# A graph and attention layer on one core: keys and queries from raw rows laid out by feature, earlier edge visits, and the last chunk's node sums kept on the chip

## The chip, the cores and the metric

The kernel runs on one core of a Trainium2 chip. The metric is the time of one execution on the device in microseconds (us), the median of several runs. All data are float32.

## What is computed

There are 10,000 nodes with 512 features, and 160,000 edges sorted by their destination. Of the reference, what matters:

```python
xn = layernorm(x)
# node sums
h = xn @ W;  msgs = h[src] * edge_weight[:, None]
gnn = relu(segment_sum(msgs, dst, 10000) + bias)
# linear attention, 8 heads of 64
q, k, v = split(xn @ w_qkv.T)
q = softmax(q per head) * 64**-0.5;  k = softmax(k over all nodes)
context = k.T @ v per head;  mix = gamma_layer_norm((q @ context) @ w_out.T)
x1 = x + gnn + mix
# experts: six with 341 hidden units, weighted by one router for all rows
out = x1 + sum_e weight_e * (gelu(layernorm(x1) @ W1[e] + b1[e]) @ W2[e] + b2[e])
```

`src` lists for each edge the row that is gathered, and `dst`, sorted, the node to which it is added. The kernel sums the weighted rows of `xn` first and multiplies by W after. The destinations are drawn so that low nodes have many edges and high nodes few: a tile of 128 edges covers about 16 nodes at the end of the list.

## The kernel before

**Chunks.** The nodes are cut into 19 chunks of 512 and a last one (chunk 19) of 272. A chunk lies in SBUF as 128 partitions (68 in the last) by SUB = 4 rows by 512 features. A float32 product with 512 columns is two matmul instructions in the profile.

**Start.** `normal_rows` (L411) loads chunks of x on SP's queue (L416), takes their statistics on DVE (L166, L167), finishes the factors on POOL, normalises on ACT (L422) and stores the normalised rows to `xn_d` in DRAM (L424). It is called in portions from `work`, so that all 20 chunks pass while PE does chunks 0 and 1; ROWS_IN sets the pace. After LISTS = 10 chunks, `edges_listed` (L445) loads the lists of the edges and `place_edges` (L454), a generator, computes on DVE at which row of its window each edge adds. Two of its steps follow each chunk of rows.

**Keys and queries.** The loop at L856 goes over the chunks. It needs the rows turned (features on the partitions): `turned_rows` (L837) calls `transposed` (L196), 16 transposes on PE (L201) and four evictions (L203), on ACT alone for the first two chunks and then two on ACT and two on DVE. Chunks 0 and 1 use plain products (`times`, L209). From chunk 2 on, `seven` (L246) makes keys and queries together from 28 products per chunk, with sums of the turned rows (`xs_b`, L226 to L229) and of the weights (`kq_sum`, L233 to L236). ACT takes the exponentials (L885, L896 to L901) with the factor `usable`, which is 1 when a test of the weights' norms holds (`norms`, `as_they_are`). Then 16 products `pc` (L911) add the keys' transposed rows times the normalised rows into `G` (L914, L918), and the queries are turned (16 transposes) and stored as `qT_d`. The rows for `pc` are loaded again from `xn_d` (`rows_of`, L834).

**Edge visits.** The 1250 edge tiles belong to 866 windows of 32 node rows, four windows to a group, 217 groups. The first 384 windows have two tiles each (groups 0 to 95), the others one. `edges_in` (L573) issues one gather of 128 rows per tile on POOL (L583) and builds `sel` on DVE (L589, L591). `edges_summed` (L595) does a visit: eight or four products of 32 output rows each into one bank (L601), a copy on ACT (L604) and one store of 128 rows to `part_d` on ACT's queue (L605). Windows overlap in up to four rows, which `carry` (L672) adds from each window to the next by accumulating transfers within DRAM on POOL's queue (L673). The order of PE's instructions is written out by hand: `work(us)` counts the nominal time of the products done and calls `edges_to` for as many tiles as PACE = 0.9 us (later ROW_PACE = 0.96 us) allows. The count starts at -16 tiles when chunk 2 begins. Gathers use a ring of 24 buffers. The other engines' order comes from a scheduler that goes by a cost model; `behind` adds to it that one instruction comes after another.

**Node rows.** Behind a short stage that forms the matrix `mix`, the loop at L1063 goes over the chunks again. `attention` (L1038), three chunks ahead (MIXED = 3), multiplies queries with `mix` (`po`), takes a layer norm and adds x. `gathered` (L1013) fetches a chunk's node sums from `part_d` with an indirect transfer on POOL (L1017); which windows have to be carried by then is in AT_HAND. The sums are turned (`aT`), multiplied with W (`pg`), and bias, relu and the sum follow on DVE (L1089, L1090). When chunk 16 calls `gathered(17)`, groups 207 to 210 are forced; chunk 17 begins with `all_edges_in` (L1005), which forces groups 211 to 216, carries the last windows and releases the edges' memory; then come the attention of chunk 19 and the rest.

**Experts.** `experts_weights` (L293) loads their weights on SP, `sums_of_weights` (L379) adds parts of them on DVE. The first chunk's normalised and turned rows are made while chunk 18 is worked on (`rows_in`, L351, L367, and the sums `xs`, L233 to L236). From the first expert product (L243) to the end PE runs without the edges.

A second path for edge lists that do not fit these windows (`general_path`, L710) is taken when a count of good edges, made with `place_edges`, is short of its full value.

## Time and profile before

| | us |
|---|---|
| median of 3 runs | 3510.95 (3510.28 to 3531.97) |
| the profiled execution | 3518.48, of which its span 3516.7 |
| start, to the first product of chunk 2 | 160 |
| keys and queries of chunks 2 to 19, to the last product of `seven` | 1024 |
| end of that, general path's test, `mix`, first attention | 159 |
| node rows of chunks 0 to 16 | 673 |
| node rows to the end, forced visits, to the first expert product | 127 |
| experts | 1374 |

The profiled execution was on its own run, 7.5 us above the median. Start and end of a stage are read from PE's timeline. "Busy" is the time in which an engine executes; issuing a transfer is not counted. In a row of a group, the number after the bar is the idle time of the engine just before these instructions, with what ended it; "issue" is idle time for which the profile shows no wait.

### The profile page before, as it was taken

Reading aid. Unit: us, or ns where it says so; the run is one execution under the profiler, and the core shown is the slowest. Engines: PE = TensorE matmul, PEld = TensorE weight load, DVE = VectorE, ACT = ScalarE, POOL = GpSimd, SP = SyncE. Lnnn points to the kernel's source line nnn. Section 1 sums busy time; section 2 is a strip of 40 time slices with the busy share of each in tenths; the row PEclk is TensorE's granted clock in tenths of the full one; section 3 lists DMA queues with packets and bytes.
Section 4 is the critical chain, followed back from the end, with each engine's and each line's share of the span. In section 5 each row is a group of like instructions: output and inputs, shape, how many; then the busy total and the mean of one; then the engine's idle time right before and its main releaser. Section 6 shows DMA issues by size and latency. Waiting matters only on the chain. (4 is left out here: it accounts for less than half of the span.)

```text
span 3516.7 us, 36142 instructions
## 1 busy us (share of the span) xinstructions
PE 3256.7 (93%) x12819; PEld 1916.0 (54%) x12819; DVE 1766.5 (50%) x3902; ACT 831.1 (24%) x1674; POOL 1311.2 (37%) x1421
## 2 busy tenths in 40 slices
PE   6899998988999989898998988999999999999998
PEld 3433333333333333333333335888888888888886
DVE  6644445444444425564565557445445544544542
ACT  5321212121112112121222113222222222222221
POOL 3466666665666656676676630000000000000000
PEclk8999999999999979899999988999999999999999
DMA  9677777776777878898998882221212212122111
GB/s 392 235 217 249 227 247 248 254 223 208 227 223 243 247 275 318 313 332 293 318 336 301 294 268 61 60 75 58 60 57 76 60 49 84 49 60 73 60 37 38
DMA packets 216735, 654.39 MB, mean 186 GB/s; under 512 B 34425, under 2 KB 74361, under 8 KB 188831
## 3 DMA queue, kind: packets, MB, share of 16 engines
q0 software_dynamic: 104096, 354.29, 32.0%
q1 hardware_dynamic: 69992, 175.33, 15.2%
q10 hardware_dynamic: 42452, 122.31, 9.0%
q8 instruction: 105, 1.72, 0.2%
q14 instruction: 90, 0.74, 0.1%
HBM read 491.21 MB, written 166.63 MB: 187 GB/s over the span
## 5 line engine op out<-in xcount | busy, mean ns | idle before, releaser
L583 POOL DMA_INDIRECT msg<-xn_d,src_sb x1250 | 1229.9, 984 | 634.4 <-issue 287.2
L601 PE MATMUL pm<-msg,sel 128*32 128x512 f32 x2504 | 351.7, 617 | 54.5 <-issue 44.5
L911 PE MATMUL pc<-xn,ek 128*128 128x512 f32 (+1 forms) x640 | 306.5, 624 | 20.5 <-issue 15.0
L209 PE MATMUL po<-G,qT 128*128 128x512 f32 (+1 forms) x640 | 302.0, 613 | 13.0 <-issue 12.2
L209 PE MATMUL pg<-wq,aT 128*128 128x512 f32 (+1 forms) x640 | 301.3, 617 | 10.2 <-issue 9.0
L604 ACT COPY part<-pm 128x512 f32<-128x512 f32 x217 | 127.1, 586 | 733.9 <-PE pm L601 276.0
L601 PEld LDWEIGHTS pm<-msg,sel 128*32 128x32 f32 x2504 | 66.1, 110 | 302.7 <-issue 266.2
L209 PEld LDWEIGHTS pg<-wq,aT 128*128 128x128 f32 (+1 forms) x640 | 117.7, 192 | 195.7 <-issue 184.7
L911 PEld LDWEIGHTS pc<-xn,ek 128*128 128x128 f32 (+1 forms) x640 | 122.7, 199 | 177.4 <-issue 164.7
L209 PEld LDWEIGHTS po<-G,qT 128*128 128x128 f32 (+1 forms) x640 | 117.4, 191 | 185.6 <-issue 181.4
L243 PE MATMUL px<-xnT,w_sb 128*128 128x256 f32 (+1 forms) x800 | 204.6, 379 | 6.8 <-DVE u L1290 6.8
L243 PE MATMUL p<-kq_sum,xs_b 128*128 128x512 f32 (+1 forms) x432 | 201.4, 600 | 3.2 <-issue 2.4
L166 DVE BATCH_NORM_STATS2 st<-ot 128x6 f32<-128x512 f32 (+1 forms) x160 | 110.3, 689 | 178.5 <-issue 119.2
L243 PE MATMUL px<-w_sb,hh 128*128 128x256 f32 (+1 forms) x800 | 185.7, 379 | 0.0
L243 PE MATMUL py<-xs,w_sum 128*128 128x256 f32 (+1 forms) x800 | 185.3, 374 | 0.0
L243 PE MATMUL p<-wk,xnT 128*128 128x512 f32 (+1 forms) x288 | 148.1, 637 | 34.9 <-issue 26.7
L243 PE MATMUL py<-w_sum,hh 128*128 128x256 f32 (+1 forms) x800 | 179.2, 379 | 0.0
L589 DVE TENSOR_TENSOR sel<-iota_w,place 128x128 f32<-128x128 f32 (+2 forms) x217 | 74.5, 344 | 206.1 <-remote 86.2
L243 PEld LDWEIGHTS px<-xnT,w_sb 128*128 128x128 f32 x800 | 150.7, 192 | 29.9 <-DVE u L1290 10.0
L243 PEld LDWEIGHTS py<-w_sum,hh 128*128 128x128 f32 (+1 forms) x800 | 150.0, 188 | 22.7
L243 PEld LDWEIGHTS px<-w_sb,hh 128*128 128x128 f32 (+1 forms) x800 | 150.0, 188 | 22.7
L243 PEld LDWEIGHTS py<-xs,w_sum 128*128 128x128 f32 x800 | 149.8, 190 | 19.9
(298 smaller groups left out, 4577.4 us busy)
## 6 DMA issues: line engine op xcount, KB each, us to landing
part_d<-part ACTq DMA_DIRECT2D x217, 256.0 KB
msg<-xn_d,src_sb POOLq DMA_INDIRECT x1250
xn<-in_x SPq DMA_DIRECT2D x19, 1024.0 KB
xn_d<-xn ACTq DMA_DIRECT2D x19, 1024.0 KB
qT_d<-qT ACTq DMA_DIRECT2D x19, 1024.0 KB
qT<-qT_d SPq DMA_DIRECT2D x19, 1024.0 KB
xt<-in_x SPq DMA_DIRECT2D x19, 1024.0 KB
x_d<-ot SPq DMA_DIRECT2D x19, 1024.0 KB
```

The costliest lines, as they stand in the source:

```text
L166: nc.vector.bn_stats(st[:r, s, :], t[:r, s, :])
L209: nc.tensor.matmul(po[:r, :], t[:, kb, s * r : (s + 1) * r], w[:, kb, :], start=kb == 0, stop=kb == KB - 1)
L243: nc.tensor.matmul(o, lhs[j], rhs[j], start=start and j == 0, stop=stop and j == n - 1, skip_group_check=True)
L583: nc.gpsimd.indirect_dma_start(out=m[k], out_offset=None, in_=xn_d, in_offset=bass.IndirectOffsetOnAxis(ap=src_sb[:, t0 + k : t0 + k + 1], ...
L589: nc.vector.tensor_tensor(sel[:, :n], iota_w[:, None, :].to_broadcast([P, n, WIN]), place[:, t0 : t0 + n, None].to_broadcast([P, n, WIN]), ...
L601: nc.tensor.matmul(pm[h * WIN : (h + 1) * WIN, :], sel[:, k, :], m[k] if k < len(m) else m[0], start=j == 0, stop=j == batch - 1, skip_gro ...
L604: nc.scalar.copy(part, pm)
L911: nc.tensor.matmul(pc, ek[:r, s, cb * P : (cb + 1) * P], xn[:r, s, :], start=s == 0, stop=s == SUB - 1)
```

## The change

- The turned rows are no longer made on PE. The host hands in x a second time, laid out by feature and chunk (`x_t`), and a chunk's turned raw rows are one load of 1 MB on SP (`turned_rows`), into the same single buffer. Raw rows give the right products because the weights are centred on the chip (`centred`: four products with a matrix of ones and four DVE instructions for each of the two), and because ACT's factor becomes the row's own one over its deviation (`rate`, `rates`).
- At the start the keys' weights and the first turned rows are loaded ahead of x; ROWS_IN is 2.0, LISTS 18. The steps of `place_edges` no longer follow the chunks of rows: the first comes after the last statistics, one later step after the last softmax of chunk 1. The reload of chunk 2 comes after the last load of x. The count of visits starts at -11 tiles.
- Windows from 384 on store 24 rows instead of 32: one transfer per window, four per group. The eight rows left out are cleared once, at chunk 5 (`rest_cleared`, 16 transfers). The test of the edges follows (USED).
- The gather of node sums is put after the last asked gather of edges (`behind`).
- Groups 211 to 216 keep their sums in SBUF (`parts`); those from 214 on are not stored. Chunk 19's node sums are made by products of these with a matrix that says which row belongs to which node (`numbered`, `last_sums`): four groups after chunk 17, two groups and the gathered rows (zeros, unless the general path ran) in chunk 19. The last carry ends at window 853.
- The attention of chunk 19 comes at chunk 16, as the distance of three has it, with visits beside it. After chunk 17 come the last groups, and then the experts' first rows are loaded ahead of their weights. The sums of the experts' weights come after the first rows are turned and before chunk 19's bias.

The diff, cut to its core:

```diff
+USED = 24
-ROWS_IN = 1.6
-LISTS = 10
+ROWS_IN = 2.0
+LISTS = 18
+FIRST_SUMS = 4
-           (17, 788), (18, 820)]
+           (17, 788), (18, 820), (19, 853)]
...
+        def turned_rows(c):
+            xnT = b_io.tile([P, KB, SUB * P], F32, name="xnT")
+            nc.sync.dma_start(xnT[:, :, : SUB * chunks[c][1]], columns(x_t, c))
+            return xnT
+
+        def centred(w):
+            pcol = psum.tile([P, D], F32, name="pcol", tag="ps")
+            for kb in range(KB):
+                nc.tensor.matmul(pcol, all_ones, w[:, kb, :], start=kb == 0, stop=kb == KB - 1)
+            for kb in range(KB):
+                nc.vector.scalar_tensor_tensor(w[:, kb, :], pcol, -1.0 / D, w[:, kb, :], op0=ALU.mult, op1=ALU.add)
...
+        nc.sync.dma_start(wk, w_qkv_t[:, D : 2 * D].rearrange("(k p) d -> p k d", p=P))
+        xnT = turned_rows(0)
+        nc.sync.dma_start(wq, w_qkv_t[:, :D].rearrange("(k p) d -> p k d", p=P))
+        squared = [squares_of(wk, "qT"), squares_of(wq, "xs_b")]
+        centred(wk)
         normal_rows(2)
...
-            nc.scalar.dma_start(part_d[i * P : (i + 1) * P, :], part)
+            if batch > 1:
+                nc.scalar.dma_start(part_d[i * P : (i + 1) * P, :], part)
+            elif i < STORED:
+                for h in range(GROUP):
+                    nc.scalar.dma_start(by_window[i * GROUP + h, :USED, :], part[h * WIN : h * WIN + USED, :])
...
+        def rest_cleared():
+            zero = pools["w"].tile([P, PER, D], F32, name="none", tag="on", bufs=1)
+            nc.gpsimd.memset(zero, 0.0)
+            for w in range(PAIRED, STORED * GROUP, P):
+                end = min(w + P, STORED * GROUP)
+                for q in range(USED, WIN, PER):
+                    nc.scalar.dma_start(by_window[w:end, q : q + PER, :], zero[: end - w])
...
-            nc.sync.dma_start(xn[: chunks[c][1]], tokens(xn_d, c))
+            load = nc.sync.dma_start(xn[: chunks[c][1]], tokens(xn_d, c))
+            if c == KEPT:
+                behind(load, last_load[0])
...
-                for _ in placing[0]:
-                    pass
+                for step in placing[0]:
+                    if step:
+                        behind(step, last_softmax[0])
-                done[1] = -16 * PACE
+                done[1] = -11 * PACE
...
-                            nc.scalar.activation(o[:r, at, :], po[:r], AF.Exp, scale=usable[:r])
+                            nc.scalar.activation(o[:r, at, :], po[:r], AF.Exp, scale=rate[:r, at : at + 1])
...
             if c + 1 == EARLY:
                 normal_rows(NCH)
+                behind(next(placing[0]), last_stats[0])
                 xn_next = rows_of(c + 1)
             if c + 1 < NCH:
-                xnT = turned_rows(c + 1, xn_next)
+                xnT = turned_rows(c + 1)
...
+        def last_sums(o, mine, groups, at):
+            n = SUB * chunks[-1][1]
+            for kb in range(KB):
+                kbs = slice(kb * P, (kb + 1) * P)
+                pt = psum.tile([P, SUB * P], F32, name="pt", tag="ps")[:, :n]
+                for g in groups:
+                    nc.tensor.matmul(pt, parts[g // 3][:, g % 3, kbs], mine[:, g].rearrange("p s n -> p (s n)"),
+                                     start=g == groups[0], stop=at is None and g == groups[-1], skip_group_check=True)
+                if at is None:
+                    nc.scalar.copy(o[:, kb, :n], pt)
+                    continue
+                r = chunks[-1][1]
+                for s in range(SUB):
+                    nc.tensor.matmul(pt[:, s * r : (s + 1) * r], at[:r, s, kbs], ident[:r, :r],
+                                     start=False, stop=s == SUB - 1, skip_group_check=True)
+                nc.vector.tensor_tensor(o[:, kb, :n], o[:, kb, :n], pt, ALU.add)
...
+            behind(sums, held["asked"])
...
-            if c == NCH - 3:
-                all_edges_in()
-                ats += [gathered(c + 1), gathered(c + 2)]
-            if c + MIXED < NCH - 1:
+            if c + MIXED < NCH:
                 mixed.append(attention(c + MIXED, nodes_rows))
-            elif c == NCH - 3:
-                mixed.append(attention(NCH - 1, nodes_rows))
+            elif c < NCH - 1:
+                nodes_rows()
             else:
-                nodes_rows()
+                last_sums(aT, mine, range(FIRST_SUMS, NQ - ON_CHIP), at)
...
+            if c == NCH - 3:
+                limit[0] = ON_CHIP + FIRST_SUMS
...
             if c == NCH - 3:
-                sums_of_weights()
+                mine = numbered()
+                aT_last = io.tile([P, KB, SUB * P], F32, name="aT_last", tag="ot", bufs=MIXED + 2)
+                edges_to(limit[0])
+                last_sums(aT_last, mine, range(FIRST_SUMS), None)
+                rows_first = all_edges_in()
```

## The prediction

> **What bounds the kernel now.** I read the page first, then busy time by stage, then the groups of PE instructions, then PE's timeline at the two places where it stands still, and there POOL's and SP's.
>
> The page: PE is the engine.
>
> ```profile
> PE 3256.7 (93%) x12819; PEld 1916.0 (54%) x12819; DVE 1766.5 (50%) x3902; ACT 831.1 (24%) x1674; POOL 1311.2 (37%) x1421
> DMA  9677777776777878898998882221212212122111
> ```
>
> The busy time by stage (columns: window, its length, then busy us of PE, PEld, DVE, ACT and POOL, granted clock, DMA share, GB/s). I cut at the first product of chunk 2 (160), the last chunk's key products (1184), the first chunk with node sums (1343), the node products of the 17th chunk (2016) and the first expert product (2143):
>
> ```profile
> 0.00:160.00 160.00, 111.43 (x339) 58.98 (x340) 105.78 (x301) 81.48 (x117) 52.75 (x102) 0.86 0.80 318
> 160.00:1184.00 1024.00, 939.22 (x3396) 384.80 (x3394) 478.72 (x961) 198.51 (x321) 664.64 (x684) 0.97 0.75 235
> 1343.00:2016.00 673.00, 620.41 (x2141) 234.34 (x2144) 382.87 (x993) 139.95 (x270) 462.86 (x464) 0.96 0.90 314
> 2016.00:2143.00 127.00, 97.35 (x337) 39.20 (x330) 82.18 (x183) 24.52 (x56) 35.76 (x76) 0.88 0.76 229
> 2143.00:3517.00 1374.00, 1351.62 (x6146) 1145.85 (x6145) 660.44 (x1338) 360.71 (x866) 0.00 (x0) 0.99 0.19 58
> ```
>
> PE idles 48.6 us before 160 and 29.7 us between 2016 and 2143, much more per us than elsewhere. The last 1374 us are the experts, full and not touched. In the key stage the removed instructions are one row (window 184 to 1184), and their 33.4 us busy and 3.8 us idle belong to PE, the bound:
>
> ```profile
> L201 PE MATMUL pt<-ident,xn 128*128 128x128 f32 (+1 forms) x272 | 33.4, 273 | 3.8 <-issue 3.8
> L911 PE MATMUL pc<-xn,ek 128*128 128x512 f32 x544 | 256.5, 614 | 20.5 <-issue 15.0 <-DVE sel L591 1.7 <-DVE G L914 1.6
> ```
>
> The start, PE's timeline (start, length, in brackets the idle time before and who ended it): long stalls, all for the turned rows or for VectorE:
>
> ```profile
> 13.28 0.47 PE L201 MATMUL pt<-ident,xn 128*128 128x128 f32 x1 [13.28 <-ACT xn L422]
> 31.72 5.91 PE L209 MATMUL pk<-wk,xnT 128*128 128x512 f32 x8 [13.29 <-ACT xnT L203]
> 51.99 0.56 PE L632 MATMUL pn<-n_small,all_ones 128*128 128x1 f32 x2 [5.94 <-DVE mv L167]
> 100.73 0.90 PE L201 MATMUL pt<-ident,qt 128*128 128x128 f32 x3 [13.32 <-DVE G L918]
> ...
> 159.87 1.88 PE L243 MATMUL p<-kq_sum,xs_b 128*128 128x512 f32 x4
> ```
>
> Behind it, in the timelines of POOL and of SP's queue: the gathers start when the last chunk of `xn_d` is stored, and SP issued the last x load only after the reload of chunk 2 (L834), which waited for a buffer until 113.89:
>
> ```profile
> 149.77 1.26 POOL L583 DMA_INDIRECT msg<-xn_d,src_sb  x1 [13.24 <-DMA xn_d<-xn]
> ...
> 113.89 0.33 SPq L834 DMA_DIRECT2D xn<-xn_d  x1
> 114.33 0.82 SPq L416 DMA_DIRECT2D xn<-in_x  x1
> ```
>
> The end, again PE's timeline: the last ten groups are forced in two heaps, each waiting for gathers or for the copy of a sum, and then the experts wait for VectorE:
>
> ```profile
> 2029.07 1.49 PE L601 MATMUL pm<-msg,sel 128*32 128x512 f32 x8 [2.47 <-ACT part L604]
> 2033.89 1.93 PE L601 MATMUL pm<-msg,sel 128*32 128x512 f32 x8 [3.32 <-issue]
> 2057.26 1.93 PE L601 MATMUL pm<-msg,sel 128*32 128x512 f32 x8 [3.65 <-issue]
> 2064.32 4.15 PE L601 MATMUL pm<-msg,sel 128*32 128x512 f32 x24 [5.12 <-ACT part L604]
> 2142.57 2.04 PE L243 MATMUL px<-xs,w_sum 128*128 128x256 f32 x4 [13.68 <-DVE xs L235]
> ```
>
> **What the Trainium skill says.** "DMA: Bandwidth & Descriptors", the section on why a DMA increments its semaphore by 16: a transfer runs on the largest k up to 16 that divides its slowest dimension, and on the hardware path on the lowest-numbered k engines. 24 rows give k = 12: two rows per engine and transfer, eight per group of four transfers, which is what 128 rows over 16 engines give. So engines 0 to 11 are relieved of nothing by the smaller stores; the trace of before has no 24-row store to show it. The same page, queues and rings: each DMA engine goes round between the queues that have work, so the burst of clearing stores shares with the gathers and does not stop them. "TensorE: Matmul & The Clock Gate", Part 1: an idle window halves the clock. The trace agrees: 0.86 granted before 160 and 0.88 in the end stage against 0.99 for the experts. Same page, the spec table: ACT and DVE queues are strict FIFO, so what stands ahead in them delays PE's evictions; the 13.32 us for G's copy, whose product had ended at 87.4, show it.
>
> **The change part by part**, against the profiled execution (3518.5 us, span 3516.7).
>
> Raw rows by feature, key stage. Out go 16 transposes per chunk (1.8 us by the timeline) and four evictions of about 0.6 us, half ACT's, half DVE's. By the row above that is 37.2 us of PE for 17 chunks. In comes one 1 MB load per chunk on SP. Its buffer is free when the seven products of the chunk end; until the next chunk PE has 16 `pc` products (13.8 us), 16 `qt` transposes (1.8) and a visit or two (1.9 each): 17 to 19 us. The load I estimate at 7 to 10 us, by the 6.5 to 7.8 us that the `z_d` stores of the same size take in the chain of waits, plus contention; the four `xs_b` sums after it are 2.7. It fits; on SP nothing that PE needs sooner stands behind it. If the cover were gone, PE would wait for the rest of it in each of 18 chunks. It adds 18 MB in 1024 us, 18 GB/s on 235, so the DMA share goes from 0.75 to about 0.81. POOL issues a gather per 1.25 us (2000.33, 2001.58 and on in its timeline). A chunk takes 58.4 us (270.76 to 329.11) and asks for 40.6 tiles (36.5 us of nominal work at 0.9 each), 50.8 us of POOL; at 56.3 a chunk it still has slack. I take 34 us of the 37 (bounds 15 and 42).
>
> Start. PE no longer waits for a row chunk, its statistics, its normalisation and 16 transposes: it needs the keys' weights and the turned rows, the first loads now. The first load landed at 7.5 us, so PE starts near 8 instead of 32. PE's work to 160, summed from the timeline, is 114 us; less 8.5 of transposes, plus 7 for centring (8 products of 0.86 us): 112. From 8 this ends at 120; the norm test (6) and two waits for VectorE to centre (3 each) make 132. VectorE's queue stands against it: 105.8 us busy before 160, and the placing of the edges (some 20 us in its timeline) now comes after the last statistics, just where `kq_sum` and `xs_b` are needed. If all of that placing comes first, chunk 2 starts at 146; I take 138, a gain of 22 (bounds 10 and 32). The gathers have to start sooner too, as visits come five tiles (4.5 us of work) earlier: the last x load no longer stands behind L834, and I expect the first gather at 135 to 143.
>
> Late stores. Four issues on ACT of 0.33 us instead of one, 118 groups (96 to 213): 0.98 us more per group, 116 us of ACT's queue in the row stage, where ACT is busy 140 of 673 us. PE has six banks between itself and ACT and two for visits, 4.6 us apart, so I take 0, with bounds of -5 and +25. Bytes saved, 7.7 MB, are written instead as 16 clearing stores of 512 KB at chunk 5: 20 us of all engines at 390 GB/s, a quarter of which is spare. I take +3 (0 to 10).
>
> End. Chunk 19's attention now comes one chunk earlier with its visits beside it, so by the pacing rule groups 207 to 214 fall between products and only 215 and 216 are forced. Of 29.7 us idle I let 24 go, and 2 of the slow clock (`pg` took 16.0 us at 2035.75 against 13.9 at 2083.93). New on PE: 24 products of 272 columns at 0.857 x 272/512 = 0.46 us, 10.9; the ones that add the gathered rows, 2.4 against the 1.2 of the transposes they replace. Sum: 26 less, 12 more: -14 (bounds -24 and +4). Late next is VectorE, with about 19 us of work (turning 2.3, sums 2.8, weight sums 6, statistics) against 21 of PE. The wait of chunk 18 for its gathered rows hides the carry (6.1 us from issue to the gather) and the gather behind 10 us of products and 7.3 of the first node sums.
>
> Sum: -34 - 22 + 0 + 3 - 14 = -67: 3451.5 in the profile. The profiled execution was 7.5 us above the median of the runs, 3510.95, so the forecast is 3444.
>
> **Rivals.** (1) The key stage gives nothing: PE waits there for something else at the same rate (it idles 8% there, mostly "issue"), and the extra DMA traffic slows gathers. For: DMA share up, POOL at 87% of its rate. Against: the row stage idles the same 8% at a share of 0.90. Then -36 + 3 = -33: 3478. (2) Slower: ACT's queue. Place: the row stage; four issues per group ahead of the copies of `po`, `aT` and `part`. If 0.9 us of each group's 0.98 reached PE, it would be +106 - 67: 3550. It beats the gain from 0.57 us per group, and is a loss of over 1% from 0.87. Against: ACT idles 79% there. (3) More: the start at 128, all of the end's idle time gone, the stalls of the key stage shrunk with fewer evictions: -105, 3406. (4) It doesn't do what it says: one row past the 24th in a late tile would send the kernel down the general path, thousands of us. I worked out the reference's edges: the highest place in a late tile is 23 (rows 0 to 23), so it isn't taken.
>
> **How the numbers follow.** Forecast 0.60, (1) 0.17, (2) 0.07, (3) 0.15, (4) 0.01. The range drops the slower case and takes in (1) and (3): 3404 to 3488. One per cent, about what a measurement tells from no change, is 35 us: the forecast, (3) and two fifths of (1) are faster, the rest of (1) the same, with some of the forecast's spread: faster 0.81, same 0.12, slower 0.07.
>
> **What would show it.** No `pt<-ident,xn` row; PE's count near 12,580 (336 transposes out, 96 products in). First product of chunk 2 near 138, first gather by 143. The key stage near 990 us. Row stage within 10 of 673. No idle over 6 us between the node products of chunk 17 and the first expert product. Wrong if PE waits at the seven products for the turned rows (the load isn't hidden), if `aT` or `part` copies appear as releasers in the row stage, or if PE idles over 15 us before chunk 2 for `place` or `xs_b`.

## The result, and the profile after

The kernel after takes 3550.6 us (median of 10 runs, 3537.67 to 3556.44), the kernel before in the same comparison 3518.61 (3507.34 to 3531.97): a ratio of 1.0085, 95% interval 1.0064 to 1.0106. A second comparison gave 1.0074 (1.0050 to 1.0098). The forecast was 3444. The runs that follow were spread over several chips: the kernel before takes 3510 to 3522 on most of them and 3299 on one, so every time stands beside the kernel before of its own comparison. Where one run of a kernel is all there is, the text says so.

The profiled execution of the kernel after took 3556.44 us with a span of 3554.6; before it was 3518.48 and 3516.7. The page, the lines that answer to those of before:

```profile
PE 3245.7 (91%) x12579; PEld 1895.3 (53%) x12579; DVE 1744.4 (49%) x3905; ACT 803.5 (23%) x1630; POOL 1308.3 (37%) x1424
DMA  9587777887777778899898865212112122122111
```

PE has 240 instructions fewer, as counted ahead, but only 11.0 us less busy time. The busy time by stage, cut at the first product of chunk 2, at the seven products of chunk 19, at the first node product, at the node products of chunk 15 and at the first expert product (columns as before: window, length, busy us of PE, PEld, DVE, ACT, POOL, granted clock, DMA share, GB/s):

```profile
0.00:173.00 173.00, 114.77 (x306) 58.80 (x307) 113.25 (x333) 76.44 (x107) 40.19 (x98) 0.82 0.79 314
173.00:1221.00 1048.00, 917.04 (x3125) 356.63 (x3124) 459.24 (x923) 180.86 (x288) 675.69 (x692) 0.94 0.78 255
1401.00:2044.00 643.00, 594.67 (x2033) 223.19 (x2034) 353.14 (x943) 128.67 (x254) 439.03 (x442) 0.96 0.90 305
2044.00:2177.00 133.00, 123.86 (x441) 54.84 (x441) 81.94 (x190) 26.21 (x59) 46.86 (x87) 0.96 0.73 209
2177.00:3555.00 1378.00, 1351.49 (x6146) 1145.22 (x6144) 668.95 (x1361) 360.29 (x867) 0.00 (x0) 0.99 0.20 60
```

The start is longer (173 us against 160) and the key stage is longer (1048 against 1024), at a lower granted clock (0.82 against 0.86, and 0.94 against 0.97), although PE has fewer instructions in both (306 against 339, 3125 against 3396). The row and end stages can't be read off against the windows of before: their cuts at 1343 and 2016 lie ahead of the first node product (1359.0) and among the node products of chunk 15, which begin at 2002.7.

For all that follows I cut every kernel at the same five places of PE's timeline: the first of chunk 2's seven products, that of chunk 3, the first node product (`pg`) of chunk 0, that of chunk 15, and the first expert product. "Stretch" is the time from chunk 3 to the first node product; it holds the key stage from chunk 3 on and the short stage that forms `mix`. Row stage and end follow. us:

| kernel, profiled execution | chunk 2 starts | chunk 2 | stretch | row stage | end |
|---|---|---|---|---|---|
| before | 159.9 | 50.5 | 1148.6 | 643.7 | 139.9 |
| before, once more (b_again) | 160.2 | 49.7 | 1139.4 | 646.1 | 138.8 |
| after | 173.0 | 65.4 | 1162.5 | 642.9 | 133.0 |
| after, once more (after_again) | 174.3 | 67.1 | 1146.3 | 649.9 | 127.5 |

b_again and after_again ran beside each other. Against before, the two pairs say: start +13 and +14, chunk 2 +15 and +17, stretch +14 and +7, row stage -1 and +4, end -7 and -11, experts +4 and +2. Of the stages, only the end is shorter in both pairs.

PE's timeline at the start of the kernel after (start, length, in brackets the idle time before and who ended it):

```profile
80.95 0.45 PE L217 MATMUL pt<-ident,qt 128*128 128x128 f32 x1 [10.62 <-DVE stats L183]
...
157.19 0.45 PE L217 MATMUL pt<-ident,qt 128*128 128x128 f32 x1 [15.69 <-DVE qt L210]
...
173.03 1.88 PE L259 MATMUL p<-kq_sum,xs_b 128*128 128x512 f32 x4
...
217.91 4.52 PE L985 MATMUL pc<-xn,ek 128*128 128x512 f32 x6 [17.77 <-ACT ek L969]
```

PE does start at 9.8 us, and has the keys and queries of chunk 0 by 63. What it gained it gives back at the query transposes of chunks 0 and 1, which wait for the softmax on VectorE (24.4 and 20.5 us in four waits each, of which the first is shown). In chunk 0 the softmax stands in VectorE's queue behind the statistics of rows that are still being loaded; in chunk 1 behind the placing of the edges, which now begins after the last statistics. The queues of SP and POOL show why rows and gathers are late:

```profile
63.50 0.33 SPq L457 DMA_DIRECT2D xnT<-in_x_t  x1
...
147.40 1.32 POOL L626 DMA_INDIRECT msg<-xn_d,src_sb  x1 [0.19 <-issue]
173.77 0.96 POOL L626 DMA_INDIRECT msg<-xn_d,src_sb  x1 [25.05 <-DVE count L557]
```

The turned rows of chunk 1 have to wait for the one buffer until chunk 0's products end, and the loads of x stand behind that wait on SP. The first gather comes at 147, and the second 26 us later: the message buffers lie where the placing's temporaries were, and the last of these is read by L557. Chunk 2's first visit then waits for its messages, and the copies and exponentials queued behind it hold PE for 17.8 us at 217.91.

In the key stage, the row of the removed transposes is gone, and the idle time has moved to `pc`. The same group in both kernels, from the seven products of chunk 3 to those of chunk 19 (busy, mean ns, then idle before and its releasers), before and after:

```profile
L911 PE MATMUL pc<-xn,ek 128*128 128x512 f32 x512 | 242.4, 615 | 20.5 <-issue 15.0 <-DVE sel L591 1.7 <-DVE G L914 1.6
```

```profile
L985 PE MATMUL pc<-xn,ek 128*128 128x512 f32 x513 | 251.1, 633 | 52.9 <-issue 21.8 <-ACT ek L969 14.2 <-ACT ek L970 10.2
```

The end is as drawn up, with one stall above the 6 us that I allowed:

```profile
2111.51 5.52 PE L225 MATMUL pg<-wq,aT 128*128 128x512 f32 x8 [6.32 <-DVE ot L1201]
...
2129.56 7.50 PE L1114 MATMUL pt<-mine,parts 128*128 128x272 f32 x32
...
2176.80 1.03 PE L259 MATMUL px<-xs,w_sum 128*128 128x256 f32 x4
```

### The profile page after: what moved, and what is told of

The parts are those of the page before. It is cut to its first block, busy times and chain, and to the rows that moved or that the text cites. A ratio compares the mean times of both kernels' runs of the same rounds, so it can differ in the third digit from the quotient of the medians.

```text
span 3554.6 us, 36005 instructions
## 1 busy us (share of the span) xinstructions
PE 3245.7 (91%) x12579; PEld 1895.3 (53%) x12579; DVE 1744.4 (49%) x3905; ACT 803.5 (23%) x1630; POOL 1308.3 (37%) x1424
## 4 chain that ended last, share of the span: by engine, by line
PE 53%; DMA 4%; issue 3%; DVE 2%; another core or an unknown queue 1%; ACT 0%; ACTq 0%; SPq 0%; DVEq 0%
PE px L259 14%; PE pz L259 10%; PE py L259 9%; PE po L225 7%; PE pg L225 7%; PE pm L644 3%; PE ph L259 2%; DMA z_d<-xt 1%; PE pt L217 1%; DMA xt<-x_d 1%; DMA xt<-in_x 0%; DMA xn<-x_d 0%; DMA w_sb<-in_w 0%; DVE xt L1460 0%
## 5 line engine op out<-in xcount | busy, mean ns | idle before, releaser
L644 PE MATMUL pm<-msg,sel 128*32 128x512 f32 x2504 | 342.9, 610 | 26.9 <-issue 22.9
L225 PE MATMUL po<-G,qT 128*128 128x512 f32 (+1 forms) x640 | 309.2, 626 | 12.3 <-issue 11.3
L225 PE MATMUL pg<-wq,aT 128*128 128x512 f32 x608 | 285.8, 615 | 15.1 <-issue 7.3
L259 PE MATMUL px<-xnT,w_sb 128*128 128x256 f32 (+1 forms) x800 | 205.1, 379 | 12.1 <-DVE u L1398 12.1
L225 PEld LDWEIGHTS pg<-wq,aT 128*128 128x128 f32 x608 | 111.9, 193 | 188.4 <-issue 167.2
```

What stands on the lines that cost most here:

```text
L225: nc.tensor.matmul(po[:r, :], t[:, kb, s * r : (s + 1) * r], w[:, kb, :], start=kb == 0, stop=kb == KB - 1)
L259: nc.tensor.matmul(o, lhs[j], rhs[j], start=start and j == 0, stop=stop and j == n - 1, skip_group_check=True)
L644: nc.tensor.matmul(pm[h * WIN : (h + 1) * WIN, :], sel[:, k, :], m[k] if k < len(m) else m[0], start=j == 0, stop=j == batch - 1, skip_gro ...
```

## Experiments

### Are the clearing stores or the small stores the loss? (a_full)

```diff
-            if batch > 1:
+            if i < STORED:
                 nc.scalar.dma_start(part_d[i * P : (i + 1) * P, :], part)
-            elif i < STORED:
-                for h in range(GROUP): ...
...
-                rest_cleared()
```

> The kernel after, with the late groups storing all 128 rows in one store and no clearing stores. Theory A (the 16 clearing stores, which run at 166 to 220 us beside the first gathers, make the messages of the first visit land late): the 17.8 us idle of PE in chunk 2 goes, the seven products of chunk 3 start some 15 us earlier than at 238.4, and the kernel takes about 3533. Theory B (the messages are late because the gathers themselves start late, the second of them at 173.8 behind the placing of the edges): chunk 2 keeps at least 12 us of its idle time, and the kernel stays within 5 us of 3550. If the four small stores per group cost something in the row stage, that stage (first node product of chunk 0 to that of chunk 15, 642.9 us) gets shorter by over 5 us; I expect within 3.

Measured: 3551.78 us, 1.0107 of before (1.0067 to 1.0147), and chunk 2 took 67.6 us with an idle 18.5 us at `pc`, as in the kernel after. Theory A falls and B holds: the clearing stores, which run beside chunk 2's products, cost nothing that can be seen, and the late messages come from the late gathers. The row stage took 636.9 us, 6.0 less than in the kernel after; the kernel after itself differs by 7.0 between two executions, so that says nothing.

### The placing as before (a_start, a_start2)

```diff
-ROWS_IN = 2.0
-LISTS = 18
+ROWS_IN = 1.6
+LISTS = 10
...
                     placing.append(place_edges(*edges_listed()))
+                for _ in range(2 if placing else 0):
+                    next(placing[0], None)
...
-                for step in placing[0]:
-                    if step:
-                        behind(step, last_softmax[0])
+                for _ in placing[0]:
+                    pass
...
-                behind(next(placing[0]), last_stats[0])
```

> The kernel after, with the placing of the edges as the kernel before has it (lists loaded at the 10th chunk, two placing steps per chunk of rows, no order behind the last statistics and the last softmax); the turned rows, the clearing and the end stay. Theory S (the placing that was moved behind the last statistics holds the softmax of chunk 1 and the message buffers): the 15.7 us wait of PE at the query transposes of chunk 1 goes, the second gather comes at about 150 instead of 173.8, chunk 2 starts at 150 to 158, and the kernel takes 3515 to 3535. Rival (the start is bound by the loads of x and the statistics, so that chunk 1 waits anyway): chunk 2 starts at 165 or later and the kernel is within 8 us of 3550.

> The earlier run with before's placing of the edges in the kernel after, again, beside the kernel after itself: 15 to 30 us less than the kernel after, of which the idle time in chunk 2 is 15; chunk 2 itself still starts at 170 to 175, because VectorE places the edges while chunk 0's softmax waits.

Measured: 3522.5 us, 1.0021 of before (1.0003 to 1.0039), and the second time 3523.35, 1.0031 (1.0013 to 1.0048), beside 1.0074 for the kernel after on the same chip: 18 us less. The gathers run without a gap from 140.7 us on, and chunk 2 takes 47.9 and 47.7 us; its idle time is gone. But chunk 2 still starts at 173.0 and 172.3. Half of theory S held: the gathers and the time, not the start. The rival was right on the start and wrong on the time: VectorE now places edges at 62 to 113 us, and PE waits 36.1 us in chunk 0 for the softmax. In both orders of the placing VectorE has the same work before chunk 2, and starting PE 22 us sooner brought nothing by itself.

### The two kernels once more, side by side (after_again, b_again)

No edit: the kernel after and the kernel before as they stand, in one comparison with a_start2.

> The kernel after, unchanged, on the same chip as the three other runs, because the kernel before took 3515 in one comparison and 3299 in another. If the loss is that of the start (chunk 2 at 173 instead of 160, its first visits 15 us late for messages) and the key stage can't repay it since the gathers set its pace, the ratio to before is 1.005 to 1.010 where before takes 3515, and 1.000 to 1.006 where it takes 3299. Rival: where gathers are quick (3299) the removed transposes count in full and the ratio falls to 0.990 or lower.

> The kernel before, unchanged, for its stage times on the chip of these runs: chunks 3 to 18 in 974 us and the row stage in 644 where the kernel takes 3515; 830 to 845 and 570 to 580 where it takes 3299.

Measured: 3541.34 us and, in one run, 3509.98, beside 3512.56 for before: the ratio of 1.0074 is in the range expected where before takes 3515. The rival speaks of the other chip and is not tested here. The stages of the table above repeat within 3 us up to chunk 2. From chunk 3 on two executions of one kernel differ by up to 16 us in the stretch, so that a difference of a few us there is not read as an effect.

### Does the removal of the transposes count without the gathers? (n_before, n_after)

```diff
-                    if k < n:
+                    if k < n and t0 + k >= 24:
+                        m[k] = kept[(t0 + k) % 24]
+                    elif k < n:
                         m[k] = pools["m"].tile([P, D], F32, name="msg")
+                        kept[(t0 + k) % 24] = m[k]
```

> The kernel before with only the first 24 of the 1250 gathers of messages; later visits multiply the messages of these 24 tiles again. All products, copies and stores stay. Theory G (in the key stage PE waits for messages, a wait that the records of PE hide): chunks 3 to 18 (973.7 us from the seven products of chunk 3 to those of chunk 19) take under 920. Rival P (PE itself is the bound there): over 950.

> The kernel after with only the first 24 gathers of messages, as in the run beside it. Theory G: chunks 3 to 18 (982.5 us in the kernel after) take 30 to 40 us less than in the kernel before without its gathers, so the removed transposes count in full once no message is waited for. Rival P (the gain was eaten by the order on ACT and DVE or by the load of the turned rows): within 12 us of the kernel before without its gathers.

Measured, in one run each: 3234.45 and 3235.65 us, where the kernel before takes 3514.8. The gathers cost 280 us, far more than any stage of the change was to bring. The stretch of both, by engine:

```profile
208.00:1175.50 967.50, 963.64 (x3764) 405.09 (x3760) 522.80 (x1065) 223.54 (x362) 5.25 (x5) 1.00 0.23 83
```

```profile
232.60:1176.60 944.00, 937.30 (x3505) 378.51 (x3503) 504.92 (x1027) 205.32 (x329) 5.26 (x5) 1.00 0.29 102
```

Without gathers PE is full and its clock is 1.00. Chunks 3 to 18 take 828.4 us before and 802.1 after: 26.3 less, short of the 30 to 40 that theory G named and well above the 12 of rival P. It is what PE's busy time in the stretch falls by (963.64 to 937.30), so the removal is worth what PE saves, once PE is what counts. Of theory G the numbers came near; that PE's loss is a wait for messages is not shown by these runs, and a later experiment speaks against it. The stretch is 23.6 shorter and the end 2.3, which pays for the start (13.9 later) and chunk 2 (10.7 longer): the change is even.

### The start as before, raw rows from chunk 2 on (a_mid, a_best)

```diff
+        normal_rows(2)
         wk = kvp.tile([P, KB, D], F32, name="wk")
...
-        xnT = turned_rows(0)
...
+        xnT = early_rows(0, xn)
...
-                xnT = turned_rows(c + 1)
+                xnT = early_rows(c + 1, xn_next) if c + 1 < EARLY else turned_rows(c + 1)
```

`early_rows` is `transposed` from the normalised rows; chunks 0 and 1 have the factor `usable` again; and the placing is that of before. a_best also centres `wq` before chunk 0's products.

> The kernel after with the start of the kernel before: chunks 0 and 1 take their turned rows from the normalised rows by 16 transposes each, rows are loaded first, the edges are placed between the statistics; raw rows by feature are used from chunk 2 on, and the weights are centred while PE waits for the first rows. Theory L (the change lost because its start puts the gathers and chunk 2 late; the key stage gains once the gathers start at 140 to 150 as before): chunk 2 starts at 157 to 163, chunks 3 to 18 take 940 to 960 us, and the kernel 3485 to 3500. Rival M (the supply of messages sets the pace of the key stage, so that nothing is gained there whatever the start): chunks 3 to 18 take 965 to 980 and the kernel 3505 to 3520.

> The earlier run with the start of the kernel before (raw rows by feature from chunk 2 on), with the weights for the queries centred too while PE waits for the first rows: chunk 2 starts at 158 to 164 instead of 168, and the kernel takes 10 us less than the run with before's placing, 0.5% to 0.9% less than before. If the start doesn't matter since the gathers set the pace from then on, it equals the run with before's placing within 4 us.

a_mid ran on the chip where before takes 3298.81: 3285.33 us, a ratio of 0.9956 (0.9940 to 0.9973). Chunk 2 started at 168.1, later than expected, and chunks 3 to 18 took 826.0. Theories L and M were put in numbers of the other chips, so this run doesn't decide between them. a_best ran on a chip where before takes 3512.56: 3521.21, 1.0037 (1.0017 to 1.0057), with chunk 2 at 166.0 and a stretch of 1140.3. So a_mid beats the kernel before by 13.5 us on the one chip, and a_best loses 8.7 to it on the other. There it equals a_start2 within 4 us, as its second expectation said: a start that is 6 us sooner is gone by the end. The kernel after itself wasn't run on the first chip, so the sign of the whole change there is open.

### What of the gathers sets the pace? (g64_before, b16, a_once; then b16_2, g64_2, a_once2)

```diff
-                            out=m[k], out_offset=None, in_=xn_d,
-                            in_offset=...(ap=src_sb[:, t0 + k : t0 + k + 1], axis=0))
+                            out=m[k][:64], out_offset=None, in_=xn_d,
+                            in_offset=...(ap=src_sb[:64, t0 + k : t0 + k + 1], axis=0))
```

```diff
-tc.tile_pool(name="edge_m", bufs=24,
+tc.tile_pool(name="edge_m", bufs=16,
```

```diff
-                xnT = turned_rows(c + 1)
+                xnT = turned_rows(c + 1) if c < EARLY else xnT
```

The first and second are edits of the kernel before, the third of a_start.

> The kernel before with each gather fetching 64 of its 128 rows and each node product multiplying those 64 rows only: as many GpSimd instructions and products as before, half of the gathered bytes and packets. If the issue of one gather per 1.25 us on GpSimd sets the supply, chunks 3 to 18 (973.7 us before, 828.4 without gathers) stay over 930. If the fetching and landing sets it, they fall under 880.

> The kernel before with 16 message buffers instead of 24. If the buffers set the supply (a gather can start only when a group of eight has been multiplied), chunks 3 to 18 take over 1030 us instead of 973.7. If the DMA's or GpSimd's own rate sets it, under 990.

> The kernel of the earlier run with before's placing (chunks 3 to 18 in 954.1 us), with the turned rows loaded for chunks 0 to 2 only; later chunks multiply those of chunk 2 again, so 17 loads of 1 MB are left out. If these loads hold up the messages or come late for the sums, chunks 3 to 18 take under 938 us. If they cost nothing, within 8 us of 954.

All three, one run each, fell on the chip where before takes 3298.81. Chunks 3 to 18 took 828.2, 843.0 and 836.4 us. With no gathers at all PE needs 828.4 for the first two and 802.1 for the third, which has no transposes. Where the gathers cost so little, these runs can't tell what of them costs. Again, one run each, on chips where before takes 3515 and 3522:

> The kernel before with 16 message buffers instead of 24, again, for a chip on which the kernel before takes 3515 (there GpSimd stays 16 gathers ahead of the group being summed). If a message can be used only some 20 us or more after its gather, chunks 3 to 18 take over 1050 us instead of 972; if PE is held up by something that the lead of the gathers doesn't touch, under 990. On a chip of the other kind: 843 again.

> The kernel before with 64 of 128 rows fetched by each gather and multiplied, again, for a chip on which the kernel before takes 3515: if bytes and packets set the pace, chunks 3 to 18 take under 900 us instead of 972; if the number of gathers does, over 950. On a chip of the other kind: 828 again.

> The same kernel with all gathers, and with the turned rows loaded for chunks 0 to 2 only (17 loads of 1 MB left out), on a chip where before takes 3515: if these loads eat the gain of the removed transposes, the stretch from chunk 3 to the first node product falls from 1143 to 1150 to under 1130; if not, it stays within 10 us of 1146. On a chip where before takes 3300, 990 again.

Measured: a stretch of 1134.3 with 16 buffers, 1161.4 with half of the rows, 1148.8 without 17 MB of turned rows, against 1139.4 and 1148.6 before and 1142.6 and 1150.1 in a_start. Chunks 3 to 18 took 973.6 with 16 buffers and 988.0 with half of the rows, as expected if neither the lead of the gathers nor their bytes set the pace. Within the 16 us by which two executions differ, neither buffers nor bytes nor the new loads set it. The part of rival (1) that blamed the extra DMA traffic is out.

### Gathers that nobody waits for (n_side, n_side_after)

```diff
+                    if k < n and t0 + k < 8:
+                        m[k] = kept[t0 + k] = ...   # gathered once, multiplied in every visit
+                    elif k < n:
+                        beside = pools["m"].tile([P, D], F32, name="msg")
+                        m[k] = kept[(t0 + k) % 8]
+                        nc.gpsimd.indirect_dma_start(out=beside, ...)
```

> The kernel before with all gathers issued, but the products multiply the messages of the first eight tiles, so that from then on neither PE waits for a gather nor a gather for PE (16 buffers that nobody reads). Theory W (PE loses its time by waiting for messages): chunks 3 to 18 take 825 to 850 us although the gathers now run at full rate, one per 1.25 to 1.4 us. Theory C (the traffic of the gathers slows PE itself, its operands or its clock): over 900 where the kernel before takes 3515.

> The same edit in the kernel after. Theory W: 20 to 30 us less in chunks 3 to 18 than in the run beside it. Theory C: within 12 us of it.

Measured, in one run each: 4742.72 and 4702.53 us, beside 3514.69 for before. Chunks 3 to 18 took 2016.5 us in n_side and 1921.2 in n_side_after. Theory W falls, and C holds in that PE itself is slowed; but its number (over 900) is left far behind, and the second run is 95 us below the first where C said within 12 and W 20 to 30. Two windows of n_side, one with gathers and one without, while GpSimd stands for 708 us in a carry that waits for the stores to `part_d`:

```profile
700.00:1000.00 300.00, 87.64 (x107) 22.25 (x108) 16.20 (x28) 6.37 (x10) 230.95 (x215) 0.50 0.68 193
1900.00:2200.00 300.00, 300.00 (x1168) 126.06 (x1161) 162.04 (x323) 67.04 (x108) 0.00 (x0) 1.00 0.19 71
```

In 300 us PE gets 107 product instructions done beside 215 gathers, and 1168 without. No product waits for a gather here. The timelines of PE and of POOL at the beginning of that:

```profile
203.65 1.01 PE L919 MATMUL pc<-xn,ek 128*128 128x512 f32 x1 [1.79 <-issue]
205.75 1.01 PE L919 MATMUL pc<-xn,ek 128*128 128x512 f32 x1 [1.09 <-issue]
208.55 1.01 PE L919 MATMUL pc<-xn,ek 128*128 128x512 f32 x1 [1.79 <-issue]
```

```profile
204.49 0.95 POOL L590 DMA_INDIRECT msg<-xn_d,src_sb  x1 [0.31 <-issue]
205.74 0.95 POOL L590 DMA_INDIRECT msg<-xn_d,src_sb  x1 [0.30 <-issue]
```

PE's idle time is put down to "issue", that is to nothing that the profile shows. The DMA engines are on average less busy (0.68) than in the row stage (0.90), which speaks against DMA engines that are full. In the kernels before and after, GpSimd pauses when the ring of 24 buffers is full: in before's stretch 137.8 us of its idle time end with a visit. In n_side, up to the carry, it is never idle for more than 0.9 us. The two engines then fall into step, here a little later, PE and POOL:

```profile
765.75 1.01 PE L919 MATMUL pc<-xn,ek 128*128 128x512 f32 x1 [1.79 <-issue]
768.55 1.01 PE L919 MATMUL pc<-xn,ek 128*128 128x512 f32 x1 [1.79 <-issue]
```

```profile
765.35 1.10 POOL L590 DMA_INDIRECT msg<-xn_d,src_sb  x1 [0.30 <-issue]
766.75 1.10 POOL L590 DMA_INDIRECT msg<-xn_d,src_sb  x1 [0.30 <-issue]
768.15 1.10 POOL L590 DMA_INDIRECT msg<-xn_d,src_sb  x1 [0.30 <-issue]
```

A product starts every 2.80 us and a gather every 1.40: one product for two gathers. From 600 to 1000 us there are 143 products beside 286 gathers, and from 1000 to 1400 again 143 and 286.

### One gather in six left out (a_45)

```diff
-                    if k < n:
-                        m[k] = pools["m"].tile([P, D], F32, name="msg")
+                    if k < n and k and (t0 + k) % 5 == 4:
+                        m[k] = newest
+                    elif k < n:
+                        m[k] = newest = pools["m"].tile([P, D], F32, name="msg")
```

An edit of a_start, with all its visits and products. Meant was one gather in five; since the first gather of a visit always stays, 207 of the 1250 are left out, one in six.

> The kernel after with before's placing of the edges (1143 and 1150 us from chunk 3's seven products to the first node product, 944 in the kernel after without gathers), with one gather in five left out; the visit multiplies the message fetched just before in its place. If each gather costs PE the same, 121 fewer of some 604 save a fifth of the 200 us: 1105 to 1115. If PE is held up only when GpSimd gets no pause, the pauses grow and the stretch falls under 1060. If the number of gathers doesn't matter, it stays over 1135. On a chip where before takes 3300 it tells less: 950 to 985.

Measured, in one run: 3280.73 us beside 3522.29 for before. The stretch of a_start and of a_45:

```profile
220.90:1363.50 1142.60, 1021.59 (x3505) 398.99 (x3503) 499.12 (x1026) 200.73 (x325) 743.21 (x760) 0.94 0.78 258
```

```profile
216.10:1204.70 988.60, 955.61 (x3504) 380.92 (x3502) 498.53 (x1026) 201.66 (x329) 620.18 (x626) 0.98 0.79 263
```

POOL has 134 instructions fewer and the stretch 154.0 us less, 1.15 us for each, at the same DMA share. That is no price per gather: all the other 621 cost only 44.6 us more (n_after, 944.0), as PE is nearly full again (955.61 of 988.60 busy). The row stage falls from 632.9 to 572.3, near the 561.8 without gathers. The second of the three expectations held (under 1060), and the first, that a gather costs PE its share of the loss, some 0.3 us, did not.

The second gave a reason: PE is held up when GpSimd gets no pause. The traces fit it. In the stretch, n_after, a_start and a_45 have the same products in the same order, so each can be set beside n_after in steps of eight products. a_start is behind by over 2 us in 31 steps of 437, which make 157 of its 199 us; a_45 in 6, which make 29 of its 45. So the loss comes in short standstills. And a_start has 30 runs of 14 or more gathers that follow each other within 2 us each, a_45 has 6. That such a run brings on the standstill is not shown by this.

## Why the prediction was wrong

Two steps failed, each worth about half of the 105 us between forecast and measurement: that PE bounds the key stage, so that its saved work is saved time (48 us), and that PE's own work sets the start (50 us).

**What bounds the kernel.** I read "PE is the engine" from its 93%, and found POOL at 87% of its rate with "still slack". Between chunk 3 and the first node product, time went with the gathers, not with PE's work: on the chips where before takes 3510 to 3522 the stretch has 755 to 760 POOL instructions in before, after, a_full, a_start, a_start2, a_once2 and a_best and lasts 1139 to 1163 us, with the transposes and without. With 626 it lasts 988.6, with next to none 944.0 or 967.5. POOL is not the bound in PE's place: at 1.25 us each, 757 instructions are 946 us of the 1148.6. PE's 93% was partly work and partly products that stood in PE without getting on: PE was busy 1042.4 us in before's stretch and 963.6 in that of n_before, which has the same products.

**Key stage, -34.** PE does save the work, and it is worth 26.3 us in chunks 3 to 18 when nothing is gathered, inside my bounds of 15 to 42. With gathers I measured +9 (973.7 to 982.5) and, in the second pair, -7 (970.9 to 964.2). This is rival (1), to which I gave 0.17: PE stays at the same rate for another reason. My reason in it, more traffic, was wrong (a_once2); the argument that I set against it, the same 8% idle at a DMA share of 0.90 in the row stage, was no argument, since the row stage loses 82 us to the gathers too (643.7 against 561.8).

**Start, -22.** This is the other step that failed: wrong by 35 us, and by 50 with chunk 2. I summed PE's work and added small waits. The worry that I named, placing in front of `kq_sum` and `xs_b`, was put at 8 us. I missed two waits: the softmax of both early chunks behind statistics and placing on VectorE (44.9 us together), and the message buffers behind the placing's last temporary (25.05 us at the second gather). "First gather by 143" was 147.40, and the second is what counted. The test I gave, "PE idles over 15 us before chunk 2 for `place` or `xs_b`", nearly met the place: 15.69 us, for the softmax behind `place`. a_start shows that the placing's order costs 18 us of the result. The other part, a start of PE that brings nothing, stays.

**Clearing, +3, late stores, 0.** Right. a_full is not faster than the kernel after, and the row stage is 642.9 and 649.9 us against 643.7 and 646.1. The row stage is within the 10 us that I allowed, though not read between the cuts of 673: my "17th chunk" at 2016 is the 16th, whose node products begin at 2002.7. My place for the clearing was wrong: the scheduler put it beside chunk 2, not at chunk 5. Rival (2), with ACT's queue as the cause of a loss at 3550, gave the measured time by luck, with a mechanism that didn't happen: in the row stage `part` shows nowhere as a releaser of PE, and `aT` once for 1.1 us, in the kernel before just the same.

**End, -14.** -6.9 and -11.3, with less DVE stall at the first expert product (13.68 us gone) and the two heaps of forced groups gone. Without gathers the end gains only 2.3, so here too part of what went was waiting that comes with the gathers. The experts, which I had called untouched, take 4 and 2 us more: their waits for `u` on VectorE grew from 6.8 to 12.1 us, in the second pair from 6.7 to 11.7.

**The sum** of -67 was to give 3451.5 in the profile, and the profiled execution took 3556.44. The 105 us between them are the start and chunk 2 (50), the stretch (48), the end (7), the experts (4), less 3 for the clearing, which I had counted by itself; the rest, 1 us, is the row stage.

## What to carry to other kernels

An engine at 93% is not shown to be the bound until something that it doesn't do is taken away: a kernel without its gathers, or with a sixth of them left out, showed in one run that PE's saved work could not count here. When work is moved behind something ("after the last statistics"), follow its memory as well as its queue: the buffers that take over the space of its temporaries move with it. And an engine that starts sooner gains little if the next engine in its chain, here VectorE with its softmax, has no room sooner.

## What the runs showed of the hardware that I had not expected

**PE hardly moves while GpSimd issues gathers without a pause.** On the chip of n_side (before: 3514.69 us) it got one product instruction done per 2.8 us (107 in 300), one for every two gathers, with a granted clock of 0.50, in a kernel in which these products wait for no gather, and returned to full speed when the gathers stopped. There, gathers of half the rows cost as much as whole ones (a stretch of 1161.4), and a ring of 16 buffers as much as one of 24 (1134.3). Why is open: the runs tell that the number of gathers matters, and perhaps how closely they follow each other, not what PE and GpSimd share.

**Chips differ in it.** On one chip the kernel before takes 3299 us, and on it a_mid's stretch has 752 POOL instructions in 982.4 us with PE's clock at 0.99; on the others 755 to 760 of them take 1139 to 1163. In a_mid 367 gathers follow each other within 2 us each, and still the stretch is only 38 us longer than that of n_after. It is one chip in one comparison, so whether the chip itself makes the difference is not shown. A kernel that overlaps gathers with products should be compared on more than one chip.

**A product's record can be far ahead of its result.** In the kernel before, PE's timeline has a visit at 975.55 and its next transposes at 977.41. The copies that take their results, on ACT and on VectorE, come some 15 us later, and PE shows little but single products with short idle times in between, at first one every 1.40 us:

```profile
983.59 0.59 PE L911 MATMUL pc<-xn,ek 128*128 128x512 f32 x1 [0.71 <-issue]
984.99 1.12 PE L911 MATMUL pc<-xn,ek 128*128 128x512 f32 x1 [0.81 <-issue]
```

```profile
992.04 0.59 ACT L604 COPY part<-pm 128x512 f32<-128x512 f32 x1 [14.58 <-remote]
```

```profile
994.16 0.69 DVE L203 COPY xnT<-pt 128x512 f32<-128x512 f32 x1 [15.49 <-PE pc L911]
```

The Trainium skill, "Perfetto Trace Analysis", in the part on the Tensor Engine instruction, says that the recorded start is that of the reading of operands and that the end is estimated from the size. This trace agrees as far as it goes: both copies had waited some 15 us, VectorE's for PE by the profile. So PE's busy time and idle time can't be added up to a bound where its products may stand still; the waits of the engines that take its results show it.
